# A first row map for the first two expert slots, ahead of the whole map of the routing

## The chip, the cores and the metric

The kernel runs on one core of a Trainium2 chip. The metric is the device time of one execution in microseconds (us). A core has a matrix engine (PE, with its weight loads shown apart as PEld), a vector engine (DVE), an activation engine (ACT), a general engine (POOL) and a queue engine (SP); each runs its own instructions in order and waits for the others on semaphores. Data comes from memory by 16 DMA engines.

## The reference

What matters here is the first stage, a mixture of experts (two of eight for each of 2048 tokens); a linear attention, an attention with a field and two local attention layers with feed-forward parts follow.

```python
x = x + attn(moe(x, cond_256))
x = x + ffn(cond2(x, cond_256))

def moe(x, genre_embed, rms_w, wg_W, wg_b, gg_W, gg_b, W1, b1, W2, b2, W3, b3):
    var = jnp.mean(x * x, axis=-1, keepdims=True)
    xn = rms_w * (x * jax.lax.rsqrt(var + EPS))
    gate = xn @ wg_W + wg_b + (genre_embed @ gg_W + gg_b)
    gate_w = jax.nn.softmax(gate, axis=-1)
    topk_w, topk_i = jax.lax.top_k(gate_w, TOP_K)
    cw = jnp.sum(jax.nn.one_hot(topk_i, E) * topk_w[..., None], axis=-2)
    h1 = jax.nn.relu(jnp.einsum('bsh,ehm->bsem', x, W1) + b1)
    h2 = jax.nn.relu(jnp.einsum('bsem,emn->bsen', h1, W2) + b2)
    out_e = jnp.einsum('bsen,enh->bseh', h2, W3) + b3
    return jnp.einsum('bseh,bse->bsh', out_e, cw)
```

x is 4 x 512 x 256, all in 32-bit floats; the experts are 256 to 512 to 512 to 256.

## The kernel before

The kernel doesn't compute every expert for every token. It sorts the 4096 choices (2048 tokens, two choices k each) into slots, each of one or two rows of 128 tokens of one expert, and runs the slots one after another (18 that always run, `often`, and 6 under a condition).

*Routing.* After the gate's products (PE, to 16.9 us) DVE finds the two choices of each token, counts them by expert, and works out for every choice its place: `slots`, split into `hl`, the place's upper part (`hl[:, 0]`, which 64 rows) and lower part (`hl[:, 1]`, which of the 64). `eid` holds the expert of each slot. The *row map* turns this around: for each place, the token that sits there. It is made by PE as a product of one-hots, in four groups of four tiles of 128 tokens (lines 1412 to 1432): on DVE `ol` (L1417, comparing the lower part with 0 to 63) and `oh` (L1422, comparing the upper part with 0 to 79), then `ol` is multiplied by the token's number, for k = 0 on ACT (L1426), for k = 1 on DVE (L1427). PE multiplies `ol` (its 64 columns are the weights) with `oh` (80 columns moving) and sums over the tiles into `pmap`; k = 0 goes to the rows 0 to 63 of the result and k = 1 to 64 to 127. Then the sum is copied (L1434), folded over k by PE (`mfold`, L1437), and turned into `rowtok`, token numbers (L1439, L1440), and `goal`, where results are to be written (L1442, L1445). `busy(n)` issues n products that nobody reads (n x 2 MATMULs of 512 columns).

*Slots.* `loads(j)` reads the expert number from `eid` on SP and starts the slot's weights: w1 (516 KB), w2 (1024 KB), w3 (640 KB); there are two buffers of each, so the first two slots' loads start at once, and slot j + 2's when slot j is done with its weights. `fetch(j)` gathers the slot's rows of x by `rowtok` with an indirect DMA on POOL, one for each 128 tokens. `turn_tokens` transposes them on PE and copies them on ACT into `xbT`. `layer` is one expert layer: products on PE into `ph`, then bias and relu, in turn on ACT (L1459) and DVE (L1461). Slot 0 has one row of 128 tokens, slot 1 two. A slot of one row makes its four quarters m = 0 to 3 of a layer in one bank and only then runs the four relus.

*The order of the work.* A framework orders the instructions and sets the semaphores. Instructions given to `pinned` (`keep_in_program_order`), and PE's inside `PE.in_order()`, keep the order of the program on their engine. In the loop over the slots, iteration j does: layer one of slot j, loads of slot j + 1, gathers of slot j + 2 (for j = 0 `xtail` too), layer three of slot j - 1, the scatters of results, the transposes of slot j + 1, layer two of slot j. Before the loop stand slot 0's loads, the gathers of slots 0 and 1, and slot 0's transposes.

Of the kernel before, what the change touches and what calls it, by code (L numbers as in the profile page):

```python
# [67 lines left out]
def adaln_attn_ffn_kernel(ctx: ExitStack, tc: tile.TileContext, a: dict, out: bass.AP):  # L68
# [1105 lines left out]
    with ExitStack() as abc:  # L1174
# [7 lines left out]
        with ExitStack() as moe:  # L1182
# [140 lines left out]
            PE.matmul(ppos[:, :128], tot, mtiles[:, :128], start=False, stop=True)  # L1323
            E2 = [128, NE, 3 * NE]
# [74 lines left out]
            nc.vector.tensor_copy(hl, hli)  # L1399
            past = per_expert("past")  # L1400
# [10 lines left out]
            nc.vector.tensor_copy(nhalf, halfs[0:1, NE - 1 : NE])  # L1411
            pmap = acct("pmap")
            for i0 in range(0, B * NT, 4):
                i1 = i0 + 4
                O4 = [128, 2, 4, 64]
                ol = hp.tile(O4, F32, tag="ob", name="ol", bufs=3)
                nc.vector.tensor_tensor(  # L1417
                    ol, hl[:, 1, :, i0:i1].unsqueeze(3).to_broadcast(O4),
                    miota[:, :64].unsqueeze(1).unsqueeze(1).to_broadcast(O4), ALU.is_equal)
                H4 = [128, 2, 4, NHI]  # L1420
                oh = hp.tile(H4, F32, tag="h1", name="oh")
                nc.vector.tensor_tensor(  # L1422
                    oh, hl[:, 0, :, i0:i1].unsqueeze(3).to_broadcast(H4),
                    miota.unsqueeze(1).unsqueeze(1).to_broadcast(H4), ALU.is_equal)
                for i in range(i0, i1):
                    nc.scalar.mul(ol[:, 0, i - i0, :], ol[:, 0, i - i0, :], mtok[:, i : i + 1])  # L1426
                nc.vector.tensor_tensor(  # L1427
                    ol[:, 1], ol[:, 1], mtok[:, B * NT + i0 : B * NT + i1].unsqueeze(2).to_broadcast([128, 4, 64]), ALU.mult)
                for i in range(i0, i1):
                    for k in range(2):  # L1430
                        PE.matmul(pmap[64 * k : 64 * k + 64, :NHI], ol[:, k, i - i0, :], oh[:, k, i - i0, :],
                                  start=(i == 0), stop=(i == B * NT - 1))
            half_map = xp.tile([128, NROWT, 2], F32, tag="hmap", name="hmap")
            nc.vector.tensor_copy(half_map, pmap[:, :NHI].rearrange("p (r q) -> p r q", q=2))  # L1434
            pmap2 = acct("pmap2")
            for q in range(2):
                PE.matmul(pmap2[64 * q : 64 * q + 64, :NROWT], mfold, half_map[:, :, q], start=True, stop=True)  # L1437
            rowtok = xp.tile([128, NROWT], I32, tag="rowtok", name="rowtok")
            nc.vector.tensor_scalar(rowtok, pmap2[:, :NROWT], -1.0, 0.0, ALU.add, ALU.max)  # L1439
            nc.vector.tensor_single_scalar(rowtok, rowtok, B * S - 1, op=ALU.bitwise_and)  # L1440
            goalf = xp.tile([128, NROWT], F32, tag="goalf", name="goalf")
            nc.vector.scalar_tensor_tensor(goalf, pmap2[:, :NROWT], 0.0, maside.to_broadcast([128, NROWT]),  # L1442
                                           ALU.is_equal, ALU.mult)
            goal = xp.tile([128, NROWT], I32, tag="goal", name="goal")
            nc.vector.tensor_tensor(goal, pmap2[:, :NROWT], goalf, ALU.add)  # L1445


            def busy(n):
                with PE.in_order():
                    ps = mmt("pbusy")  # L1450
                    for _ in range(n):
                        PE.matmul(ps, ident, xres[0].rearrange("p t h -> p (t h)")[:, :512], start=True, stop=True)


            busy(4)
# [12 lines left out]
            def loads(j, d):  # L1468
                e = nc.sync.value_load(eid[j : j + 1, 0:1], min_val=0, max_val=NE - 1)
# [16 lines left out]
            def fetch(j, d):  # L1486
                d.xb = hp.tile([128, 2, H], F32, tag="xb", name="xb", bufs=3)
                for i in range(d.n):
                    r = place(d.n, SLOTS[j][0]) + i
                    pinned(nc.gpsimd.indirect_dma_start(  # L1490
                        out=d.xb[:, i, :], out_offset=None, in_=xall,
                        in_offset=bass.IndirectOffsetOnAxis(ap=rowtok[:, r : r + 1], axis=0)))
# [30 lines left out]
            def layer(d, src, tag, w, bias):  # L1523
# [4 lines left out]
                for m2 in range(d.n):  # L1528
                    ps = mmt("ph")
                    k = 4 // d.n  # L1530
                    for i in range(k):
                        m = m2 * k + i
                        mm(ps[:, i * n : (i + 1) * n],
                           [(w[:, c, m * 128 : (m + 1) * 128], src[:, c, 0:n]) for c in range(w.shape[1])])
                    if d.n == 2:
# [135 lines left out]
            fetch(0, ds[0])  # L1671
            fetch(1, ds[1])
            with PE.in_order():
                turn_tokens(ds[0])
            last_wide = max(j for j, d in enumerate(ds) if d.wide)
            often, rare = ds[:-NRARE], range(len(ds) - NRARE, len(ds))
            for j, d in enumerate(often):
# [9 lines left out]
                with PE.in_order():  # L1687
                    if d.few:
                        h1 = layer_few(d, d.xbT, d.t1, "h1", w1, d.s1, 0)
                    else:  # L1690
                        h1 = layer(d, d.xbT, "h1", w1, 0)
                    if j + 1 < len(often):
# [11 lines left out]
                    if j == 0:  # L1704
                        pinned(nc.gpsimd.indirect_dma_start(
# [370 lines left out]
```

## Time and profile before

| | us |
|---|---|
| time, median of 3 runs (1340.82 to 1342.1) | 1341.5 |
| the profiled execution | 1343.32 |
| its span, first to last instruction | 1341.6 |
| PE busy in the span | 1271.8 |
| hl made (DVE) | 30.5 |
| slot 0's w1, w2, w3 started | 29.98, 30.55, 31.08 |
| slot 1's w1, w2, w3 started | 32.20, 32.79, 33.32 |
| map's products (PE) | 32.15 to 38.2 |
| filler on PE, busy(4) | 38.76 to 42.46 |
| gathers issued on POOL: slot 0, slot 1 (two), slot 2 (two), xtail | 39.58, 40.92, 42.20, 43.45, 44.70, 45.95 |
| slot 0's transposes, first layer, second layer | 45.21, 46.11, 49.42 |
| slot 1's first layer | 53.65 |

The profile is of one execution. Times in it count from the span's start. In the chain of waits each line is a start, a length, and the engine and line whose work the end hung on; a transfer's length there runs from its issue to its landing. An engine's idle time costs only where it is in this chain. PEclk is the clock granted to PE, 1.00 or 0.50 in this profile. A product of 32-bit floats shows as two MATMULs.

### The profile page before, as it was taken

What the parts mean: (1) busy time and instruction counts of PE and PEld (TensorE: products, weight loads), DVE (VectorE), ACT (ScalarE), POOL (GpSimd) and SP (SyncE); (2) the same over time, 40 slices, a digit from 0 to 9 for tenths busy, and PEclk for the clock granted to TensorE, in tenths of its full rate; (3) what the DMA queues carried; (4) which work ended last, traced back from release to release, by engine and by line L of the source; (5) the groups of instructions that cost most, each with busy time, mean ns of one, the idle gap of its engine ahead of it and who ended that gap; (6) DMA issues with size and microseconds to landing.
All of it is one profiled execution on the core that took longest, in us unless ns stands there. A gap on an engine that the chain in (4) does not pass through costs nothing.

```text
span 1341.6 us, 23073 instructions
## 1 busy us (share of the span) xinstructions
PE 1271.8 (95%) x9214; PEld 812.2 (61%) x9214; DVE 683.4 (51%) x1464; ACT 581.4 (43%) x1157; POOL 292.9 (22%) x321
## 2 busy tenths in 40 slices
PE   4899999998999999999999999999999998999998
PEld 3788899964566634344344655766555556667654
DVE  6221243425777733242237788654372877864421
ACT  3221233326655365646644646561222655463111
POOL 1322356420000101010103334210030333422010
PEclk7899999998999999999999999999999999999999
DMA  3565666523000000000210001311001011012000
GB/s 96 213 236 192 236 239 221 189 76 116 1 1 1 1 1 1 0 1 1 91 57 14 18 18 27 104 34 25 24 0 43 25 30 30 18 43 56 18 21 22
DMA packets 41856, 85.29 MB, mean 64 GB/s; under 512 B 9409, under 2 KB 25673, under 8 KB 39433
## 3 DMA queue, kind: packets, MB, share of 16 engines
q1 hardware_dynamic: 36600, 73.02, 16.9%
q0 software_dynamic: 3504, 9.46, 2.1%
q8 instruction: 77, 1.26, 0.4%
q10 hardware_dynamic: 1632, 1.21, 0.3%
q14 instruction: 43, 0.34, 0.1%
HBM read 74.76 MB, written 6.82 MB: 61 GB/s over the span
## 4 chain that ended last, share of the span: by engine, by line
PE 75%; DVE 9%; DMA 6%; ACT 5%; issue 3%; POOL 1%; SPq 0%; DVEq 0%; POOLq 0%
PE ph L82 11%; PE pdq L82 7%; PE pfy L82 6%; PE sc L82 6%; PE pua L82 5%; PE pug L82 5%; PE pv L82 5%; PE pdy L82 4%; PE po L82 3%; PE pn L82 3%; DMA ys<-ob,goal 2%; PE pds L82 2%; PE pqk L82 1%; PE pz L82 1%; PE pqt L86 1%
## 5 line engine op out<-in xcount | busy, mean ns | idle before, releaser
L82 PE MATMUL pdq<-wqkv,yT 128*128 128x512 f32 x384 | 171.7, 597 | 2.4 <-DVE t L626 2.2
L424 ACT ACTIVATE cex<-sc 128x512 f32<-128x512 f32 x256 | 132.2, 604 | 85.6 <-PE sc L82 84.6
L82 PEld LDWEIGHTS pdq<-wqkv,yT 128*128 128x128 f32 x384 | 71.1, 190 | 84.6 <-issue 76.1
L82 PE MATMUL ph<-h,w 128*128 128x256 f32 (+2 forms) x576 | 121.5, 370 | 0.3 <-ACT h L1596 0.3
L629 POOL TENSOR_TENSOR qr<-t,t 128x512 f32<-128x512 f32 x64 | 81.3, 1271 | 140.5 <-DVE t L626 140.5
L82 PEld LDWEIGHTS ph<-h,w 128*128 128x128 f32 x576 | 102.0, 192 | 15.2 <-ACT h L1596 0.5
L1461 DVE TENSOR_SCALAR h<-ph,w 128x256 f32<-128x256 f32 (+2 forms) x52 | 23.0, 461 | 121.8 <-PE ph L82 101.7
L394 POOL TENSOR_SCALAR fterm<-vw,faT 128x256 f32<-128x256 f32 x16 | 14.6, 920 | 317.6 <-DVE cr L384 317.6
L82 PE MATMUL sc<-qm,kT 32*128 32x512 f32 x512 | 82.6, 639 | 0.0
L681 ACT ACTIVATE p<-pds,ss 128x192 f32<-128x192 f32 (+1 forms) x256 | 79.8, 425 | 2.1 <-PE pds L82 0.8
L82 PE MATMUL pua<-hT,w 128*128 128x512 f32 x160 | 75.3, 593 | 0.9 <-DVE z L706 0.9
L82 PE MATMUL pug<-hT,w 128*128 128x512 f32 x160 | 76.2, 598 | 0.0
L619 ACT ACTIVATE sq<-pdq 128x512 f32<-128x512 f32 x64 | 38.5, 601 | 83.7 <-POOL qr L629 42.2
L714 POOL TENSOR_TENSOR p<-p 128x192 f32<-128x192 f32 x64 | 42.4, 682 | 138.1 <-PE pn L82 135.3
L796 ACT ACTIVATE gl<-pug,cols 128x512 f32<-128x512 f32 x40 | 27.3, 687 | 93.6 <-PE pug L82 90.8
L82 PE MATMUL pv<-cex,v 128*32 128x512 f32 x512 | 61.9, 598 | 2.7 <-DVE vw L391 2.7
L82 PE MATMUL pfy<-w,uA 128*128 128x256 f32 x256 | 61.4, 383 | 0.0
L82 PE MATMUL po<-w,h 128*128 128x256 f32 x264 | 60.1, 380 | 0.0
L82 PE MATMUL pdy<-wo,oT 128*128 128x256 f32 x256 | 58.9, 383 | 0.0
L684 DVE TENSOR_TENSOR p<-p,lmask 128x384 f32<-128x384 f32 x64 | 47.0, 735 | 23.0 <-ACT p L681 21.6
L82 PE MATMUL pn<-p,v 64*64 64x128 f32 (+1 forms) x1792 | 50.3, 254 | 8.2 <-DVE p L687 4.2
L1459 ACT ACTIVATE h<-ph,w 128x256 f32<-128x256 f32 (+2 forms) x52 | 22.4, 455 | 81.9 <-PE ph L82 78.0
(352 smaller groups left out, 2329.8 us busy)
## 6 DMA issues: line engine op xcount, KB each, us to landing
w<-in_moe_w_dram SPq DMA_DIRECT2D x18, 1024.0 KB, 7.9
w<-in_moe_w_dram SPq DMA_DIRECT2D x18, 516.0 KB, 4.0
w<-in_moe_w_dram SPq DMA_DIRECT2D x14, 640.0 KB, 4.5
zb<-rows SPq DMA_DIRECT2D x32, 256.0 KB, 4.1
g<-ys SPq DMA_DIRECT2D x6, 512.0 KB, 6.9
wqkv<-in_f_wqkv_dram SPq DMA_DIRECT2D x2, 1536.0 KB
w<-in_f_w_dram SPq DMA_DIRECT2D x2, 1408.0 KB
w<-in_moe_w_dram SPq DMA_DIRECT2D x4, 512.0 KB
```

Source lines behind the costliest of these rows:

```text
L82: cls._queue(nc.tensor.matmul(*args, **kw))
L86: cls._queue(nc.tensor.transpose(*args, **kw))
L394: nc.gpsimd.tensor_scalar_mul(fterm[:, t, :], vw, W["faT"][:, t, b : b + 1])
L424: nc.scalar.activation(ex[:, i, :], pss[2 * j + i], AF.Exp, scale=CHD**-0.5)
L619: nc.scalar.activation(sq, p3, AF.Square)
L629: nc.gpsimd.tensor_tensor(qr_t[:, s], t1, t2, ALU.add)
L681: nc.scalar.activation(p[:, j * 192 : j * 192 + n], pss[j // 2][r][:, j % 2 * 192 : j % 2 * 192 + n], AF.Exp, scale=d.ss[:, j, 1, 2 * c + ...
L684: nc.vector.tensor_tensor(edges, edges, lmask[:, :128].rearrange("p (s q) -> p s q", q=64).unsqueeze(1).to_broadcast([128, 3, 2, 64]), ALU ...
L714: nc.gpsimd.tensor_tensor(p[:, 1:, 0:64], p[:, 1:, 0:64], p[:, : NT - 1, 128:], ALU.add)
L796: nc.scalar.activation(gl, pg, AF.Gelu, bias=col("bg", l * (NU + 1) + i))
L1459: pinned(nc.scalar.activation(dst, src, AF.Relu, bias=bias))
L1461: pinned(nc.vector.tensor_scalar(dst, src, bias, 0.0, ALU.add, ALU.max))
```

## The change

- A *small map* is made first, for the three rows of slots 0 and 1 alone. `oh0` compares the upper part with the six values of these rows (two comparisons) and is itself multiplied by the token numbers, so that the lower one-hots `ols` can be used unscaled. `ols` is now made whole (four comparisons of 512 elements), in y[1] and y[3]. 32 products of six columns, k alternating, then copy, fold, `early_rows`, and the three gathers of slots 0 and 1.
- The *whole map* follows: `full_onehots` for the four groups (upper one-hots, scaling of `ols` in place on ACT and DVE), then the products of three groups, then slot 0's transposes, then those of the fourth group. Its copy stands before the loop, and the fold, `rowtok` and `goal` behind slot 0's first layer (`full_rows`), so the gathers of slot 2 and of `xtail` come after that.
- Almost all instructions of both maps are pinned to the program's order.
- `eids` is a copy of `eid` that depends on `early_rows` and stands behind the last whole-map one-hot on DVE; all slots but slot 0 read their expert from it, so their loads start behind it.
- Filler: `busy(7)` behind the counting products, `busy(2)` and `busy(1)` among the whole map's products; `busy(4)` goes.
- Slot 1's transposes move into slot 0's second layer, behind its third quarter.

```diff
@@ -1321,6 +1321,14 @@
 pcnt = mmt("pcnt")
 PE.matmul(pcnt[:, :NE], tot, mtiles[:, 128:], start=True, stop=True)
 PE.matmul(ppos[:, :128], tot, mtiles[:, :128], start=False, stop=True)
+def busy(n):
+    with PE.in_order():
+        ps = mmt("pbusy")
+        for _ in range(n):
+            PE.matmul(ps, ident, xres[0].rearrange("p t h -> p (t h)")[:, :512], start=True, stop=True)
+busy(7)
 E2 = [128, NE, 3 * NE]
 over = xp.tile(E2, F32, tag="over", name="over")
 nc.vector.tensor_tensor(over, pcnt[:, :NE].unsqueeze(2).to_broadcast(E2),
@@ -1397,6 +1405,7 @@
 nc.vector.tensor_single_scalar(hli[:, 1], slots, 63, op=ALU.bitwise_and)
 hl = xp.tile([128, 2, 2, B * NT], F32, tag="hl", name="hl")
 nc.vector.tensor_copy(hl, hli)
 past = per_expert("past")
 nc.vector.scalar_tensor_tensor(past, pairs, mslot[:, 0:1], mwt, ALU.is_le, ALU.mult)
 nc.vector.scalar_tensor_tensor(past, halfs, mslot[:, 1:2], past, ALU.is_le, ALU.add)
@@ -1409,50 +1418,98 @@
 nc.vector.tensor_scalar_min(eid, eidf, float(NE - 1))
 nhalf = xp.tile([1, 1], I32, tag="nhalf", name="nhalf")
 nc.vector.tensor_copy(nhalf, halfs[0:1, NE - 1 : NE])
+def one_hot(out, of, iota):
+    shape = list(of.shape) + [iota.shape[1]]
+    for _ in of.shape[1:]:
+        iota = iota.unsqueeze(1)
+    tc.keep_in_program_order(nc.vector.tensor_tensor(
+        out, of.unsqueeze(len(of.shape)).to_broadcast(shape), iota.to_broadcast(shape), ALU.is_equal))
+first = [2 * NPAIR + SLOTS[0][0], 2 * SLOTS[1][0], 2 * SLOTS[1][0] + 1]
+oh0 = y[2].rearrange("p t h -> p (t h)")[:, : 12 * B * NT].rearrange("p (k i n) -> p k i n", k=2, n=6)
+for at, r, n in ((0, first[0], 2), (2, first[1], 4)):
+    one_hot(oh0[:, :, :, at : at + n], hl[:, 0], miota[:, 2 * r : 2 * r + n])
+tokens = mtok.rearrange("p (k i) -> p k i", k=2)
+pinned(nc.vector.tensor_tensor(
+    oh0, oh0, tokens.unsqueeze(3).to_broadcast([128, 2, B * NT, 6]), ALU.mult))
+ols = [y[k].rearrange("p t h -> p (t h)").rearrange("p (i n) -> p i n", n=64) for k in (1, 3)]
+for i0 in (0, B * NT // 2):
+    for k in range(2):
+        one_hot(ols[k][:, i0 : i0 + B * NT // 2], hl[:, 1, k, i0 : i0 + B * NT // 2], miota[:, :64])
+def map_products(pmap, n, onehot, k, tiles):
+    for i in tiles:
+        PE.matmul(pmap[64 * k : 64 * k + 64, : 2 * n], ols[k][:, i, :], onehot(k, i),
+                  start=(i == 0), stop=(i == B * NT - 1))
+def map_copied(pmap, n):
+    half_map = xp.tile([128, n, 2], F32, tag=f"hmap{n}", name="hmap")
+    pinned(nc.vector.tensor_copy(half_map, pmap[:, : 2 * n].rearrange("p (r q) -> p r q", q=2)))
+    return half_map
+def map_rows(half_map, n):
+    pmap2 = acct("pmap2")
+    for q in range(2):
+        PE.matmul(pmap2[64 * q : 64 * q + 64, :n], mfold, half_map[:, :, q], start=True, stop=True)
+    rowtok = xp.tile([128, n], I32, tag=f"rowtok{n}", name="rowtok")
+    pinned(nc.vector.tensor_scalar(rowtok, pmap2[:, :n], -1.0, 0.0, ALU.add, ALU.max))
+    pinned(nc.vector.tensor_single_scalar(rowtok, rowtok, B * S - 1, op=ALU.bitwise_and))
+    return pmap2, rowtok
+def gather(dst, table, r):
+    pinned(nc.gpsimd.indirect_dma_start(
+        out=dst, out_offset=None, in_=xall,
+        in_offset=bass.IndirectOffsetOnAxis(ap=table[:, r : r + 1], axis=0)))
+with PE.in_order():
+    pmap = acct("pmap")
+    for i in range(B * NT):
+        for k in range(2):
+            map_products(pmap, 3, lambda k, i: oh0[:, k, i, :], k, [i])
+    early_rows = map_rows(map_copied(pmap, 3), 3)[1]
+xbs = [hp.tile([128, 2, H], F32, tag="xb", name="xb", bufs=3) for j in range(2)]
+gather(xbs[0][:, 0, :], early_rows, 0)
+for i in range(2):
+    gather(xbs[1][:, i, :], early_rows, 1 + i)
+eids = xp.tile([128, 1], I32, tag="eids", name="eids")
 pmap = acct("pmap")
-for i0 in range(0, B * NT, 4):
-    i1 = i0 + 4
...
-goal = xp.tile([128, NROWT], I32, tag="goal", name="goal")
-nc.vector.tensor_tensor(goal, pmap2[:, :NROWT], goalf, ALU.add)
+ohs = []
+def full_onehots(g):
+    tiles = slice(4 * g, 4 * g + 4)
+    oh = hp.tile([128, 2, 4, NHI], F32, tag=f"h{1 + g // 2}", name="oh")
+    one_hot(oh, hl[:, 0, :, tiles], miota)
+    for i in range(4 * g, 4 * g + 4):
+        pinned(nc.scalar.mul(ols[0][:, i, :], ols[0][:, i, :], mtok[:, i : i + 1]))
+    pinned(nc.vector.tensor_tensor(
+        ols[1][:, tiles], ols[1][:, tiles], tokens[:, 1, tiles].unsqueeze(2).to_broadcast([128, 4, 64]),
+        ALU.mult))
+    ohs.append(oh)
+def full_products(g):
     with PE.in_order():
-        ps = mmt("pbusy")
-        for _ in range(n):
-            PE.matmul(ps, ident, xres[0].rearrange("p t h -> p (t h)")[:, :512], start=True, stop=True)
-busy(4)
+        for i in range(4 * g, 4 * g + 4):
+            for k in range(2):
+                map_products(pmap, NROWT, lambda k, i: ohs[i // 4][:, k, i % 4, :], k, [i])
+for g in range(4):
+    full_onehots(g)
+pinned(nc.vector.scalar_tensor_tensor(eids, early_rows[:, 0:1], 0.0, eid, ALU.min, ALU.max))
+busy(2)
+for g in range(3):
+    full_products(g)
+    if g == 0:
+        busy(1)
+def full_rows():
+    pmap2, rowtok = map_rows(full_map, NROWT)
+    goalf = xp.tile([128, NROWT], F32, tag="goalf", name="goalf")
+    pinned(nc.vector.scalar_tensor_tensor(
+        goalf, pmap2[:, :NROWT], 0.0, maside.to_broadcast([128, NROWT]), ALU.is_equal, ALU.mult))
+    goal = xp.tile([128, NROWT], I32, tag="goal", name="goal")
+    pinned(nc.vector.tensor_tensor(goal, pmap2[:, :NROWT], goalf, ALU.add))
+    return rowtok, goal
 def relu(dst, src, bias):
     if turn[0]:
@@ -1466,7 +1523,7 @@
     return 2 * i if kind == 2 else 2 * NPAIR + i
 def loads(j, d):
-    e = nc.sync.value_load(eid[j : j + 1, 0:1], min_val=0, max_val=NE - 1)
+    e = nc.sync.value_load((eids if j else eid)[j : j + 1, 0:1], min_val=0, max_val=NE - 1)
     we = a["moe_w"][bass.DynSlice(e, 1)].rearrange("o p f -> (o p) f")
     d.w1 = ew.tile([128, 8 + 2 * ME], F32, tag="w1", name="w1")
     nc.sync.dma_start(d.w1, we[:, 0 : 8 + 2 * ME])
@@ -1487,9 +1544,7 @@
     d.xb = hp.tile([128, 2, H], F32, tag="xb", name="xb", bufs=3)
     for i in range(d.n):
         r = place(d.n, SLOTS[j][0]) + i
-        pinned(nc.gpsimd.indirect_dma_start(
-            out=d.xb[:, i, :], out_offset=None, in_=xall,
-            in_offset=bass.IndirectOffsetOnAxis(ap=rowtok[:, r : r + 1], axis=0)))
+        gather(d.xb[:, i, :], rowtok, r)
 def turn_tokens(d):
     n = d.n * 128
@@ -1520,7 +1575,7 @@
         relu(dst[:, m, :], ps, d.w1[:, bias + m : bias + m + 1])
     return dst
-def layer(d, src, tag, w, bias):
+def layer(d, src, tag, w, bias, between=None):
     if d.wide:
         return wide_layer(d, src, tag, w, bias)
     n = d.n * 128
@@ -1532,6 +1587,8 @@
             m = m2 * k + i
             mm(ps[:, i * n : (i + 1) * n],
                [(w[:, c, m * 128 : (m + 1) * 128], src[:, c, 0:n]) for c in range(w.shape[1])])
+            if between is not None and m == 2:
+                between()
         if d.n == 2:
             turn[0] ^= 1
         for i in range(k):
@@ -1668,10 +1725,12 @@
 btail = y[3][:, 0]
 htail = y[2].rearrange("p t h -> p (t h)")[:, 512:].rearrange("p (w c n) -> p w c n", w=NWIDE, c=4)
 loads(0, ds[0])
-fetch(0, ds[0])
-fetch(1, ds[1])
+ds[0].xb, ds[1].xb = xbs
 with PE.in_order():
     turn_tokens(ds[0])
+    full_products(3)
+with PE.in_order():
+    full_map = map_copied(pmap, NROWT)
 last_wide = max(j for j, d in enumerate(ds) if d.wide)
 often, rare = ds[:-NRARE], range(len(ds) - NRARE, len(ds))
 for j, d in enumerate(often):
@@ -1689,6 +1748,8 @@
             h1 = layer_few(d, d.xbT, d.t1, "h1", w1, d.s1, 0)
         else:
             h1 = layer(d, d.xbT, "h1", w1, 0)
+        if j == 0:
+            rowtok, goal = full_rows()
         if j + 1 < len(often):
             loads(j + 1, after)
             for name in list(later)[: (j > 1) + (j > 8)]:
@@ -1702,9 +1763,7 @@
         if j + 2 < len(often):
             fetch(j + 2, ds[j + 2])
         if j == 0:
-            pinned(nc.gpsimd.indirect_dma_start(
-                out=xtail, out_offset=None, in_=xall,
-                in_offset=bass.IndirectOffsetOnAxis(ap=rowtok[:, TAILS : TAILS + 1], axis=0)))
+            gather(xtail, rowtok, TAILS)
         if j == last_wide + 3:
             scatter_tails()
         if j:
@@ -1717,9 +1776,9 @@
         if 9 < j < 10 + B:
             pinned(nc.gpsimd.tensor_tensor(
                 xres[j - 10], xres[j - 10], row("bo").unsqueeze(1).to_broadcast([128, NT, H]), ALU.add))
-        if j + 1 < len(often):
+        if 0 < j < len(often) - 1:
             turn_tokens(after)
-        d.h2 = layer(d, h1, "h2", d.w2, 4)
+        d.h2 = layer(d, h1, "h2", d.w2, 4, None if j else lambda: turn_tokens(after))
         if d.wide:
             pinned(nc.scalar.copy(htail[:, d.at], d.h2[:, :, 256:]))
 last(len(often) - 1, often[-1])
```

## The prediction

> **What bounds the kernel now.** I read the page's engine table first: PE is busy 95% of the span, so time can only be had where PE waits or runs at a low clock. The slices' clock row shows one such place, slices 1 and 2.
>
> ```profile
> PE 1271.8 (95%) x9214; PEld 812.2 (61%) x9214; DVE 683.4 (51%) x1464; ACT 581.4 (43%) x1157; POOL 292.9 (22%) x321
> PEclk7899999998999999999999999999999999999999
> ```
>
> The chain that ended last, in order of time, tells what sets the end there.
>
> ```profile
> 30.57 0.69 DVE ol L1417
> 31.26 0.74 DVE oh L1422
> 32.00 0.33 DVE ol L1427
> ...
> 37.16 1.03 PE pmap L82 x16
> 38.19 0.02 issue
> 38.21 0.25 DVE hmap L1434
> ...
> 39.58 5.59 DMA xb<-in_x_dram,rowtok
> ...
> 46.11 2.66 PE ph L82 x16
> 48.77 0.85 PE pxb L86 x4
> 49.63 7.64 PE ph L82 x48
> ```
>
> The reader sees one line of dependence: one-hots on DVE, map products on PE, the gather of slot 0's tokens (5.59 us), and only then slot 0's first layer at 46.11. After that the chain is PE alone until 170 us, so what is won at 46.11 is kept. Third, busy time and granted clock by stretch (columns: stretch, its length, then PE, PEld, DVE, ACT, POOL busy, clock, DMA share, GB/s).
>
> ```profile
> 20.10:23.80 3.70, 2.17 (x8) 1.86 (x8) 2.61 (x12) 0.42 (x2) 0.00 (x0) 0.50 0.00 0
> 23.80:32.10 8.30, 0.00 (x0) 0.00 (x0) 8.06 (x51) 0.80 (x4) 0.00 (x0) 0.50 0.13 25
> 33.80:37.20 3.40, 3.18 (x33) 2.77 (x34) 3.40 (x7) 2.12 (x9) 0.00 (x0) 0.51 1.00 411
> 37.20:42.50 5.30, 4.92 (x28) 2.37 (x28) 0.93 (x6) 0.24 (x2) 2.31 (x3) 1.00 1.01 418
> 42.50:45.20 2.70, 0.00 (x0) 0.00 (x0) 0.00 (x0) 0.00 (x0) 2.09 (x3) 1.00 0.53 165
> 47.30:50.70 3.40, 3.40 (x19) 3.40 (x18) 0.70 (x2) 1.21 (x3) 0.00 (x0) 0.51 0.14 39
> ```
>
> PE is idle from 23.8 to 32.1, works the map at half clock, and after the idle 2.7 us before the gather lands it runs at half clock again from 47.3 to 50.7. The gather travels while the DMA engines are full (share 1.01) with two slots' weights.
>
> **The change part by part**, as times on this trace.
>
> *Small map.* After hl (ends 30.5): a 64-element and a 128-element comparison and a 192-element product. Rows: 0.29 (128 elements), 0.36 (192), the first between 0.17 (16 elements) and 0.29, so 0.23; the first two overlap by 0.08: 0.8, to 31.4. Then four 512-element one-hots at the pitch 0.61 that L1417 shows, the last taking 0.69: the first pair is ready at 32.7, the last at 33.9. 64 MATMULs of six columns follow, 32 for each half. The trace has no such shape. Nearest is pmap<-oh,ol with the same 64-column weights, also alternating: 14 MATMULs in 37.5 to 38.0 at clock 1.00, 0.036 each; the upper bound is 16 in 1.57 at clock 0.50, 0.098 (that time holds waits). I take 0.036: first half done at 33.85, second 33.9 to 35.05, plus 0.23 of the last one's own length: 35.3. Copy, fold, rowtok and its AND took 38.21 to 39.29, 1.08, to 36.4; the gather begins 0.17 after its last operand: 36.5, 3.1 earlier than 39.58.
>
> [...]
>
> *Filler.* busy(7) is 14 MATMULs from 23.8 on. At clock 1.00 the present filler has a pitch of 0.43; at 0.50 I take 0.86, twice, because ph shows 12 MATMULs in 2.35 us at 0.50 and 25 in 2.50 at 1.00. The clock rose after 3.4 us of work (33.8 to 37.2) or, counting the sparser start, 5.1 (32.1 to 37.2). So 4 to 6 of the 14 run slowly and the filler ends at 31.5 to 32.3, before the products at 32.7: no cost, and full clock for them. Without a rise it ends at 35.8 and costs its overhang.
>
> *Gather's flight.* The 33 gathers land after 2.7 / 3.3 / 6.1 us (least, median, most); this one took 5.59 among weights. Now only slot 0's weights are under way, 2.18 MB at about 410 GB/s from 31.3 on, 5.3 us, over at about 37. I take the median: landed at 39.8; bounds 39.2 and 42.6.
>
> *The whole map moves behind.* DVE stands still from 33.9 to 35.3, since the map's copy is pinned and waits for PE; everything pinned after it waits too. From 36.4 come four times 0.74 + 0.34 (L1422 and L1427 at their pitch), 4.3, to 40.7, then eids, 0.15. ACT's 16 scalings (1.06 for four, 4.2 in all) follow the small products, 35.3 to 39.5, ahead of slot 0's token copy; that isn't late. PE after the fold (35.9): busy(2) 1.7, to 37.6; first quarter of the products 16 x 0.036 = 0.6, to 38.2; busy(1) 0.86, to 39.0; second to 39.6; third, ready at 39.6, to 40.2; transposes 0.45 to 40.65, with the gather already there; the last quarter waits for DVE until 40.7 and ends at 41.4. The token copy ends at 41.1 (0.02 + 0.38 + 0.04 after the transposes). First layer: 41.4 instead of 46.11, **4.7 earlier**. DVE's 4.3 us set this, not the gather, which has about 0.4 us in hand.
>
> *Slot 0's two layers* took 46.11 to 53.65, 7.54, of which 3.4 at half clock. At full clock: 16 MATMULs x 0.11 = 1.8; then the four relus one after another (48.81 to 50.35, 1.54, 0.2 after PE) with only the fold between, because slot 1's transposes, which filled this place, move behind the third quarter of layer two. Its first quarter so ends at 3.8, then 24 x 0.11 + 4 x 0.11 = 3.1: 6.9, **0.6 less**. Without the clock's drop before, the moved transposes would be a loss of about 0.4.
>
> *Slot 1's and 2's data.* SP took 1.03 from eid to the first transfer: 41.9. w1 lands 4.0 later, 45.9, needed at 41.4 + 6.9 = 48.3. w2 (42.5) lands after 7.9, at most 10.2: 50.4 to 52.7, needed 5.6 later than slot 1's start, 53.9. POOL issues slot 2's gathers when the whole rowtok is made, behind the first layer's relus, at about 45.3 and 46.6 instead of 43.45 and 44.70, and xtail at 47.9; by the worst row the second lands at 52.7, needed at 53.5. Behind them POOL has slot 2's weight sums, due at about 54; SP has nothing until slot 2's weights. So these moves cost nothing, with margins of 2.4, 1.2 and 0.8.
>
> **Sum.** 4.7 + 0.6 = 5.3. The profiled execution took 1343.3 (span 1341.6 and 1.7 around it), so 1338.0 for it; it stands 1.8 above the median 1341.5, from which the forecast is **1336.2**.
>
> **The rivals.**
>
> *The clock drops between filler and whole map.* For: the drop at 20.1 came after 3.2 idle us, the one at 47.3 after a gap of 2.7 and sparse work; nothing here shows whether six-column products hold the clock. Against: the pause after the filler is 1.2 at most. If it halves from 34 to 41: second half 3.1 instead of 1.15, gather at 38.5, DVE done at 42.7, first layer at 43.5; 2.6 + 0.6 = 3.2 gained: 1338.3.
>
> *POOL can't issue the gathers beside DVE's one-hots.* In this trace every DVE operation that overlaps a gather's issue reads PSUM, so it is bounded: nothing, or until DVE is done at 40.7, landing 3.3 later at 44.0, first layer 44.9: 1.2 + 0.6, 1339.7. I take nothing, as the issues beside PSUM readers last 0.94 to 1.03 with and without them.
>
> [...]
>
> *Slot 1's or 2's data come late.* Each margin above spent, every further microsecond costs one: with 5 us of lateness nothing is left, 1341. Against it: all three worst rows were seen with two slots' weights under way, and now one is.
>
> *The filler gets in the way (the slower side).* It is in PE's queue ahead of the products. If the clock doesn't rise during it, it holds PE to 35.8, the products take 64 x 0.098 = 6.3, to 42.1, the gather starts at 43.5, the second filler and the quarters run at half clock and the first layer starts at about 55, 9 later, its layers 3.5 longer: 1354. The break-even is a rise at about 39: then the products end at 40.1, DVE at 45.7, the first layer starts at 46.4. Against: 14 dense MATMULs, and both rises in the trace came within 3.4 to 5.1 us of work.
>
> **How the numbers follow.** Forecast (own range 1334 to 1338) 0.60; clock drop 0.12; POOL held 0.10; late data 0.06; slower 0.12. Range 1332.8 to 1342.0: below, a clock that never drops again later; above, it takes in the gaining rivals and no loss, and leaves out the slower case with a little at either end. 0.2% is 2.7 us, what the measurement can tell from no change: faster means under 1338.8. Forecast, most of the clock drop and a third of POOL's case: 0.73. The rest of these and late data: 0.14. Slower, with a little for a queue order unlike the one read from the code: 0.13.
>
> **What would show it.** First gather issued near 36.5 and landed near 40; clock 1.00 without a break from 27 to 31 on; PE's first layer at 41 to 42; slot 1's at 48 to 49. Wrong if the gather's issue outlasts 1.1 us or flies over 5 beside the one-hots, if the granted clock shows 0.50 after 33, if PE waits for w1 or xb of slots 1 and 2, or if DVE's whole-map stretch exceeds 4.3 us.

## The result, and the profile after

The changed kernel takes **1344.86 us** (median of 21 runs, 1339.94 to 1348.62) against 1341.19 for the kernel before beside it (21 runs, 1335.94 to 1342.16): 1.0031 times as long, 95% interval 1.0022 to 1.0040. The forecast was 1336.2, faster. The profiled execution took 1347.1, its span is 1345.4.

From the page of the changed kernel, the engine table, the slices' clock row and the chain's shares by engine:

```profile
PE 1283.2 (95%) x9294; PEld 816.6 (61%) x9294; DVE 685.2 (51%) x1471; ACT 581.8 (43%) x1157; POOL 292.0 (22%) x321
PEclk8999999999999999999999999999999999989999
PE 72%; DVE 10%; DMA 9%; ACT 4%; issue 3%; POOL 1%; SPq 0%; DVEq 0%; POOLq 0%
```

PE has 80 MATMULs and 80 weight loads more. DMA holds 9% of the chain; before it was 6%: more of the end is set by transfers, though a gather was taken off it.

The chain around the change, in order of time (start, length, what):

```profile
31.34 2.42 DVE ymoe L1426 x4
33.76 0.04 issue
33.80 1.11 PE pmap L82 x30
...
35.44 3.18 PE pbusy L82 x4
38.62 1.07 PE pmap L82 x16
39.70 1.06 PE pbusy L82 x2
...
42.38 0.70 PE pmap L82 x16
43.08 2.00 PE ph L82 x16
```

The gather's wait is gone from the chain and slot 0's first layer starts at 43.08 instead of 46.11; slot 1's starts at 50.1 instead of 53.65. So the change does what it is for: 3.5 us are gained. They are still there 600 us later, and then they are lost in a part of the kernel that the change does not touch, the two local attention layers. There SP issues transfers that are waited for: `sums`, `rden`, `rows` and `zb` take the attention's sums through memory and back (8 KB each, `zb` 256 KB), `hn` brings rows of the tokens for the normalization (the one in the chain is 30 KB), and `pua` is a product that follows. The same chain there, first of the kernel before, then of the changed one:

```profile
805.89 2.36 DMA hn<-yc
...
862.99 7.96 DMA zb<-rows
...
872.93 1.99 PE pua L82 x4
```

```profile
802.05 4.13 DMA hn<-yc
...
861.02 9.29 DMA zb<-rows
...
872.28 3.63 PE pua L82 x4
...
915.49 2.87 DMA rows<-rden
```

The same transfers, issued in the same order, take longer to land (hn by 1.8 us, zb by 1.3), the rows transfer at 915 is new on the chain, and the products behind zb run at half clock. The busy table of 780 to 930 us (columns as before the change: length, PE, PEld, DVE, ACT, POOL, clock, DMA share, GB/s), first before, then after:

```profile
780.00:930.00 150.00, 144.17 (x1585) 95.97 (x1570) 108.81 (x257) 78.78 (x164) 42.34 (x45) 1.00 0.18 47
```

```profile
780.00:930.00 150.00, 142.23 (x1484) 93.97 (x1481) 104.54 (x247) 76.84 (x161) 39.23 (x43) 0.98 0.18 46
```

The mean clock is 0.98 instead of 1.00 (two falls to 0.50 of 3.4 us each, at 810.8 and 872.2), and in the same 150 us PE does 1484 MATMULs instead of 1585.

### The profile page after: what moved, and what is told of

Read it like the earlier page. It is cut to its first block, busy times and chain, and to the rows that moved or that the text cites. A ratio compares the mean times of both kernels' runs of the same rounds, so it can differ in the third digit from the quotient of the medians.

```text
span 1345.4 us, 23252 instructions
## 1 busy us (share of the span) xinstructions
PE 1283.2 (95%) x9294; PEld 816.6 (61%) x9294; DVE 685.2 (51%) x1471; ACT 581.8 (43%) x1157; POOL 292.0 (22%) x321
## 4 chain that ended last, share of the span: by engine, by line
PE 72%; DVE 10%; DMA 9%; ACT 4%; issue 3%; POOL 1%; SPq 0%; DVEq 0%; POOLq 0%
PE ph L82 11%; PE pdq L82 6%; PE sc L82 6%; PE pfy L82 5%; PE pua L82 5%; PE pv L82 5%; PE pug L82 5%; PE pdy L82 4%; PE po L82 3%; PE pn L82 2%; DMA zb<-rows 2%; DMA ys<-ob,goal 2%; PE pqt L86 2%; PE pqk L82 1%; DVE t L626 1%
## 5 line engine op out<-in xcount | busy, mean ns | idle before, releaser
L82 PEld LDWEIGHTS pn<-p,v 64*64 64x64 f32 x1792 | 45.4, 138 | 20.5 <-issue 11.5
```

Source lines behind the costliest of these rows:

```text
L82: cls._queue(nc.tensor.matmul(*args, **kw))
```

## The experiments

**What could do this.** The order of instructions of every engine is the same from slot 2 on. Three theories: *B*, the code's place: the change adds 161 instructions to PE's stream (80 + 80 and a wait), and what follows lies elsewhere against the packets of the instruction queue q8 (below). *K*, the clock: its falls last 3.4 us or a multiple of it (3.4, 6.8, 10.2 and 17.1 us in these profiles, but for the one at the end of each), and a stage that begins 4 us earlier may meet them differently. *A*, the tiles' addresses.

For B the trace has a row that the prediction did not use. Queue q8, which the page calls `instruction`, carries 77 packets of 16 KB, one for some 250 TensorE rows (MATMULs, weight loads and waits; medians of 255 and 252.5 rows from packet to packet in the two profiles, with some records missing). From that name and this count I take a packet for the fetch of a block of TensorE's code, and the expectations put a block at 256 rows; no run shows what a packet holds, and whether it costs anything is what is on trial. The DMA queues (packets, MB, share of the 16 engines) while hn is under way, in the changed kernel from 801.9 to 806.3 us, and in the first experiment from 802.3 to 804.9:

```profile
q1 hardware_dynamic: 547, 0.27, 25.4%
q8 instruction: 1, 0.02, 2.3%
q14 instruction: 1, 0.01, 0.6%
```

```profile
q1 hardware_dynamic: 539, 0.26, 41.3%
q14 instruction: 1, 0.01, 0.8%
```

One q8 packet more: it starts 0.7 us after hn's issue and takes 1.64 us.

### Moving the code, and nothing else (e1 to e4)

Products of one column, whose result nobody reads, in PE's wait of 16.8 to 21.5 us: 24 times in e1, 40 in e2 and e4, 64 in e3, four rows each. So e1 has 257 rows more than before, about one block, and e2 has 160 more, where the changed kernel has 161.

```diff
             ptot = mmt("ptot")
-            PE.matmul(ptot[:, 0:1], flat, ones, start=True, stop=True)
+            with PE.in_order():
+                for _ in range(24):
+                    PE.matmul(ptot[0:1, 64:65], ident[:, 0:1], ident[:, 0:1], start=True, stop=True)
+                PE.matmul(ptot[:, 0:1], flat, ones, start=True, stop=True)
```

> The changed kernel with 24 one-column products put into a PSUM column that nobody reads, at 16.6 us, where TensorE waits for the top-2 choice until 21.5 us: 96 rows more on TensorE (a product is two weight loads and two matmuls), so 161 + 96 = 257 rows more than before. Theory B (blocks of code): queue q8 fetches one block of 16 KB for each 256 TensorE rows in both traces; the change moves the places of these fetches by 161 of 256 rows, and they fall on the short DMAs that the local attention layers wait for (a fetch of 1.64 us at 802.8 us beside the hn load that took 4.13 instead of 2.36 us, one of 1.74 us at 860.5 beside the zb loads of 9.29 instead of 7.96 us). With 257 rows the fetches stand where they stood before, so the 4.2 us that the change is ahead at 690 us stay: 1337 us, 0.996 to 0.998 of before. Theory K (clock windows alone: a stage that starts 4 us earlier meets other windows, whatever the code): no difference from the changed kernel, 1345 us, 1.003. Theory A (addresses of the tiles): the same as K, 1345 us.

> The kernel before with 40 such products at the same place, 160 rows more on TensorE, hidden in its wait for the top-2 choice. Theory B: its code blocks end where those of the changed kernel do (161 rows more), the short DMAs of the local layers become late and the clock drops follow: 1341.2 + 6 to 8 = 1347 to 1349 us, 1.0045 to 1.006. Theory K: the local stage begins at the same time as before, so 1341 us, 1.000. Theory A: 1341 us too.

> The changed kernel with 64 such products, 256 rows: one whole block more. Control for the filling itself (its activity, its time). Theory B: the blocks end where those of the changed kernel end, 1345 us, 1.003. If the padding as such took away the loss (say by keeping the clock up at 18 us), this one would be as quick as the one with 24: 1337 us. Theories K and A: 1345 us. Should the 64 products last beyond 21.5 us, up to 1 us more in all three.

> The changed kernel with 40 such products, 161 + 160 = 321 rows, that is 65 beyond the place of before: a phase of the blocks that no kernel had yet. Theory B: some time of its own between the two, 1335 to 1348 us, with its hn, zb and rows loads late where a q8 fetch stands beside them, and not elsewhere. Theories K and A: 1345 us, as the changed kernel.

Measured beside one another (before 1338.9): the changed kernel with its code where before's lies (e1) 1336.4, ratio 0.9987, interval 0.9973 to 1.0000. The kernel *before* with its code where the changed one's lies (e2) 1346.4, 1.0057 (1.0034 to 1.0079). One whole block more (e3) 1341.0, 1.0025 (1.0009 to 1.0041), as the changed kernel. A fourth place (e4) 1338.9, 1.0007 (0.9993 to 1.0022); in its profile another hn load, at 864.6, is on the chain with 5.45 us, and a q8 packet starts 0.1 us before it.

K and A expected no difference from moving the code, and fall: e2 has the routing and tiles of before, and within 1.0 us the start of its local stage, and loses 7.5 us. Filling as such is no cure either, as e3 shows. The chain of e2 at the places shown above:

```profile
863.68 9.59 DMA zb<-rows
...
875.25 2.95 PE pua L82 x4
...
918.31 3.16 DMA rows<-rden
```

And e1's, again in the same places:

```profile
802.41 2.37 DMA hn<-yc
...
859.42 7.96 DMA zb<-rows
...
869.35 1.98 PE pua L82 x4
```

In e2 the transfers of the changed kernel have come back with the clock's fall behind them; in e1 all is as before, and the rows transfer at 915 is off the chain. In seven of the profiles, the time of the transfer on the chain and the starts of q8's packets after its issue (from the packet records; "-": not on the chain):

```
code lies as       kernel   hn             zb                    rows at 915
before's           before   2.36 none      7.96 (+5.3)           -
                   e1       2.37 none      7.96 (+6.6)           -
                   e12      2.34 none      8.61 (+5.0)           -
the changed one's  changed  4.13 (+0.7)    9.29 (-0.5, +7.6)     2.87 (+0.9)
                   e2       4.25 (+0.7)    9.59 (+1.2, +7.6)     3.16 (+0.8)
                   e3       3.96 (+0.7)    9.08 (+2.0, +7.6)     2.65 (+0.4)
                   e14      -              10.29 (+2.6, +7.8)    -
```

Rows without a fetch takes 1.40. zb is the weakest witness: it travels beside a 1536 KB weight load, and with one late fetch and no early one e7's took 9.13 and e9's 9.21. Over the chains of all 16 profiles after 690 us, hn took 2.33 to 2.42 us in the 27 cases with no q8 packet under way, and 2.84 to 5.77 in the nine with one; the two longest are e4's and e8's, issued 5.4 us after that weight load. Rows took 1.39 to 1.41 in 51 cases without and 2.65 to 3.16 in three with. But not every transfer suffers: sums took 1.69 to 1.76 in all 61 cases, 45 of them with a packet under way, and rden was longer only in the two of 25 whose packet started after its issue (2.66 and 3.03, the others 1.51 to 1.81). A late transfer is also likelier to be on the chain: off it, with its packet 2.0 us after the issue, one of the changed kernel's hn took 2.31.

Where the time goes, as the start of the same matmul less its start in the profile of before (us; columns e9, e12 and e14 are told of below):

```
start before   changed   e2      e3      e14     e1      e9      e12
  63.0          -3.47   +0.62   -1.46   -4.87   -1.63   -3.13   -4.60
 664.8          -4.21   -0.69   -1.11   -6.07   -3.15   -6.76   -9.19
 784.9          -3.85   -1.02   -2.53   -7.63   -3.48   -8.04  -10.84
 965.4          +2.36   +5.15   +0.84   -2.71   -3.57   -6.90  -10.36
1266.2          +4.22   +5.16   +0.37   -3.57   -6.30   -8.14  -13.50
```

Between 784.9 and 965.4 the four whose code lies as the changed kernel's lose 6.2, 6.2, 3.4 and 4.9 us; the others -0.1, 1.1 and 0.5, and the eight profiles that are not in the table 0.1 to 1.5. e3's clock does not fall in this stretch, so its 3.4 us are lost without the clock. The changed kernel has two falls besides (shown here), e2 and e14 one each:

```profile
872.20:875.60 3.40, 3.32 (x4) 1.51 (x5) 3.00 (x16) 1.67 (x3) 0.00 (x0) 0.50 0.03 5
810.80:814.20 3.40, 3.40 (x20) 2.85 (x19) 2.94 (x6) 3.40 (x10) 2.92 (x2) 0.50 0.32 94
```

What it loses after 965 goes with a fall of 6.8 us at 1189.6, where before has 3.4. The rows at 63 and 665 also hold each execution's own falls of the clock (near 303, for one, 10.2 us in before and 3.4 to 6.8 in the others).

### What the early gain lost (e5 to e8)

All with the code where before's lies, but for e6, whose blocks end 32 rows sooner (14 one-column products at 16.8 us; e5 has 22). e5 and e6: busy(8) for busy(7), and one more product between the halves of the small map's loop

```diff
+                return ps
...
-            busy(7)
+            filler = busy(8)
...
                 for i in range(B * NT):
+                    if i == B * NT // 2:
+                        for _ in range(1):
+                            PE.matmul(filler, ident, xres[0].rearrange("p t h -> p (t h)")[:, :512], start=True, stop=True)
                     for k in range(2):
```

> The changed kernel with its code blocks where those of before are (22 one-column products, and 8 rows more from filling: 257 rows as with 24), and with more filling around the small map: 8 filler products in place of 7 ahead of it, and one between its two halves, so that TensorE works from 31 to 34 us, where it waited for the one-hots. Step on trial: my forecast lost 1.6 us of its early gain because the clock fell to 0.50 at 35 us (first layer at 43.0 us, forecast 41.4), and with the padding, whose windows lie 1 to 2 us earlier, 6.8 us long (first layer at 44.9). If the thin stretch of the small map is what lets it fall, there is no 0.50 between 33 and 42 us now, the first layer starts at 41.5 to 42 us, and the total is 2 to 3 us under that of the kernel with 24 products alone: 0.996 to 0.997 of before. If the one-hots of the whole map on VectorE or something else make it fall, or the filling counts for nothing: a drop at 34 to 36 us as there, first layer at 43 to 45 us, 0.9987. If the filler is itself in the way (one product is 0.85 us at full clock), the small map ends later than 35.5 us and 0.5 us are lost.

> The same with 14 one-column products: 225 rows, blocks that end 32 rows sooner than before's. Theory B: the fetches move by some 32 rows, one to two us, against the short DMAs of the local layers; in the trace of the kernel with 24 this takes the fetch counted at the critical DMAs from 8 to 6, so the same or up to 2 us quicker than the one with 22, 0.994 to 0.997 of before; any late hn, zb or rows load has a q8 fetch beside its issue. Theory K: the same as with 22.

e5 1338.1, 0.9990 (0.9978 to 1.0003); e6 1338.35, 0.9989 (0.9976 to 1.0003). In e6's profile the clock stays at 1.00 from 27.2 to 300 us and the first layer starts at 42.7; in e5's it falls at 36.8 for 3.4 us, and the layer starts at 44.4. The third outcome came true as well: the product sits in the way, and the small map's last product ends at 36.2 in both, against 34.9 in the changed kernel, whose one-hots begin 0.4 us sooner. No gain in time, and what brings the clock down stays open.

e7 takes the small map's products of the first choice first, then the second's:

```diff
-                for i in range(B * NT):
-                    for k in range(2):
-                        map_products(pmap, 3, lambda k, i: oh0[:, k, i, :], k, [i])
+                for i0 in (0, B * NT // 2):
+                    for k in range(2):
+                        map_products(pmap, 3, lambda k, i: oh0[:, k, i, :], k, range(i0, i0 + B * NT // 2))
```

> The kernel with 24 products, and of the small map in each half first the eight products of the first choice, then the eight of the second, not in turn. If taking turns is what makes a product short (0.036 us a MATMUL in the changed kernel, the weights of one loading while the other runs in the other half of the array), a MATMUL and its load now take more, 0.05 us or above at full clock: 1.5 us and more in place of 1.1 for 30 of them, the small map 0.4 us or more later. If not: 0.036 us each at full clock, twice that at 0.50, and no difference in time from the kernel with 24, 0.9987.

Timelines, e7's weight loads and then the changed kernel's second half:

```profile
32.00 3.74 PEld L82 LDWEIGHTS pmap<-ymoe,ymoe 128*64 128x64 f32 x64 [1.11 <-PE pbusy L82]
```

```profile
33.80 1.01 PEld L82 LDWEIGHTS pmap<-ymoe,ymoe 128*64 128x64 f32 x30 [0.19 <-DVE ymoe L1426]
```

64 loads take 3.74 us here, 30 take 1.01 there, with the same clock until 34.5. By the starts of the single MATMULs, those of one half follow at 0.058 us (0.107 at half clock), and in the changed kernel a pair follows a pair at 0.058, 0.029 each. So taking turns halves a MATMUL's time. The map's end moves by less: eight products of one choice run while the other's one-hots are made, and counted from the first of these one-hots the map ends 0.2 us later than e1's (4.56 against 4.34 us; the clock falls in both before the end). 1340.15, 1.0001 (0.9985 to 1.0017), unclear against e1.

e8 reads all expert numbers from the first table:

```diff
-                e = nc.sync.value_load((eids if j else eid)[j : j + 1, 0:1], min_val=0, max_val=NE - 1)
+                e = nc.sync.value_load(eid[j : j + 1, 0:1], min_val=0, max_val=NE - 1)
```

> The kernel with 24 products, and all slots' weights loaded by the first table of expert numbers (eid), not by the copy that waits for the whole map's one-hots: slot 1's three loads are issued 4 to 5 us sooner. My forecast gave nothing for that wait. If it was right: slot 1's first layer and the rest at the same time, 0.9987. If the loads sooner are in the way of the small map's gathers: these land 0.5 us or more later, and slot 0's first layer with them; total up to 0.5 us more. If slot 1 waited for its weights: its first layer comes sooner, up to 0.5 us less.

1337.8, 0.9985 (0.9971 to 1.0000), as e1. But slot 1's loads go out at 32.66 instead of 42.33, and the gather is on e8's chain again:

```profile
36.66 7.48 DMA xb<-in_x_dram,rowtok
```

That is slot 0's. Of the third gather the trace tells the landing in both: 6.6 us here, 3.3 in e1, so the wait behind the one-hots is what keeps the gathers short. It shows in no total; a likely reason is that in e1 PE, with its filler at half clock, begins the first layer hardly sooner: 44.9 against e8's 45.3.

### The gain kept (e9 to e12), and two controls (e13, e14)

e9 leaves the changed kernel alone until 711 us and moves the code only there, where PE waits for the first scaled queries (in e9 `tiny` is 22 and `big` 2):

```diff
                     pt = mmt("pqt")
+                    if t == s == 0 and tiny + big:
+                        PE.pinned = True
+                        for _ in range(big):
+                            PE.matmul(pt, ident, xres[0].rearrange("p t h -> p (t h)")[:, :512], start=True, stop=True)
+                        for _ in range(tiny):
+                            PE.matmul(pt[0:1, 0:1], ident[:, 0:1], ident[:, 0:1], start=True, stop=True)
...
+                    if t == s == 0 and tiny + big:
+                        PE.pinned = False
```

> The changed kernel, whose code is its own until 711 us, and then 24 products that nobody reads (22 of one column, 2 of 512) in the place of the first local layer where TensorE waits from 711 to 715.3 us for the scaled queries: 96 rows more from there on. Theory B (the fetches of TensorE's code): the loss comes from the place of the fetches in the local layers alone, so all that the change gains until 690 us is kept (2 to 4 us, by how long the clock falls at 35 us) and 1 to 2 us come to it: 1335 to 1338 us, 0.996 to 0.9985 of before; hn at 802 us lands in 2.4 us, not 4.1, and no q8 fetch stands beside the zb loads at 860 us. If it was not the fetches in the local layers but something that the early padding changed (the clock at 18 us, the code of the routing), the loss stays: 1345 us, 1.003.

> The one before with 9 filler products ahead of the small map in place of 7 (and 22 late products in place of 24), so that TensorE works until 32.5 us, when the first half's one-hots are ready. If the pause from 30.8 to 32.1 us is what brings the clock down at 35 us, the first layer comes at 41.5 to 42 us instead of 43 to 45 us and the total is 1 to 2 us under the one with 7: 0.995 to 0.9975. If the short six-column products after it are enough to bring it down, no difference: the drop at 34 to 36 us stays, 0.996 to 0.9985. If the ninth product is in the way: the first half 0.3 us later, no gain.

> The same change with the two fillers behind the small map left out, busy(2) and busy(1) (and 27 late products): the whole map's products start when their one-hots and scalings are there, 37 to 38 us, instead of behind the filler at 38.6 to 40.5. If the filler, which takes 3.2 to 3.7 us when the clock is down, is what the path waits for: first layer at 41.5 to 42.5 us although the clock falls, total 0.5 to 2 us under the one with filler. If without it the clock falls for longer, and into slot 0's first layer: that layer, 2.0 us at full clock, takes 3 to 4 and the total is 1 to 3 us above.

> Both at once: 9 filler products ahead of the small map, none behind it, and 25 late products (23 of one column, 2 of 512), 257 rows more than before from 711 us on. If the two add up: the first layer at 41.5 to 42 us as without the filler, the code of the local layers where it does no harm, 0.995 to 0.9965 of before, the quickest so far. If the nine are of no use once the filler behind is gone: as the one without, 0.9974. If TensorE, with no filler behind the small map, keeps 0.50 into slot 0's layers (2.0 us at full clock, 4.0 at half): 0.998 to 1.000.

Against before: e9 0.9983 (0.9970 to 0.9997), e10 0.9962 (0.9948 to 0.9976), e11 0.9974 (0.9963 to 0.9985), e12 0.9964 (0.9949 to 0.9978; 1334.3 us, its profile's span 1327.7). All four are faster than before, and after 711 us none differs from the changed kernel but by the place of its code and that filling. Without the filler behind the small map (e11) the chain reads:

```profile
33.41 3.70 ACT ymoe L1492 x15
...
37.20 3.58 PE pmap L82 x48
...
41.16 0.70 PE pmap L82 x16
41.86 2.00 PE ph L82 x16
```

First layer at 41.86, 1.55 sooner than in e9, though the clock falls at 37.1 all the same: ScalarE's scalings and the products themselves set it now, not the filler, and the clock is back before the layer. The nine filler products of e10 gain nothing in the routing (first layer 43.56, the fall at 36.8 stays), so that its total lies below e9's, with overlapping intervals, is no proof for them.

Two controls ask what the late filling does by itself. e13 gives its two long products to the kernel before; e14 is e12 without the late products.

> The kernel before with the two 512-column products alone in TensorE's wait of 711 to 715 us (8 rows, so its code blocks move by 8 of 256). If the late filling itself makes the quickest kernels quick (TensorE busy there, no fall of the clock at 715 us), it gives the kernel before the same: 1 to 2 us less, 0.9985 to 0.9993 or below. If their gain is the change's with the code blocks in a harmless place: 1.000, within 0.05%.

> The quickest kernel (9 filler products ahead of the small map, none behind it) without its 25 late products: 161 + 8 - 12 = 157 rows more than before, so its code blocks end where those of the changed kernel do, and the routing is the quickest one's to the instruction. Theory B: the loss of the local layers is back, 5 to 8 us more than the quickest: 1340 to 1343 us, 1.0005 to 1.003. If the better filling of the routing made it quick and not the place of the code: 1335 to 1337 us, 0.9965 to 0.998 (the late filling's own part lost, no more).

e13 0.9997 (0.9984 to 1.0010): no gain from the filling. e14 1341.0, 1.0015 (0.9999 to 1.0031): the loss is back, 0.5% between it and e12. Its chain, then e12's:

```profile
856.25 10.29 DMA zb<-rows
...
868.53 2.67 PE pua L82 x4
```

```profile
851.99 8.61 DMA zb<-rows
...
862.57 1.98 PE pua L82 x4
```

## Why the forecast was wrong

**The step that failed** is the sentence "After that the chain is PE alone until 170 us, so what is won at 46.11 is kept". It looked 120 us ahead in a program of 1340. Later the chain runs again through short transfers that SP issues (hn, sums, rden, rows, zb), in the profile of before as well, and some of these land later when TensorE's code lies elsewhere (hn after 4.13 us instead of 2.36 in the changed kernel, 4.25 in e2). No rival held this; all four looked at the routing. The added instructions had a cost outside their own stage: 6.2 us from 785 to 965 us, in a term that the sum did not have. Shown: moving the code alone makes the loss in the kernel before (e2, 1.0057) and takes it away in the changed one (e1, 0.9987). Seen with every late hn, rden and rows on the chain, but not shown by itself: that it is the q8 packet beside a transfer that delays it. No run leaves a packet out alone. How a late transfer is followed by a fall of the clock is not shown either; e3 lost 3.4 us with none. By what path one 16 KB packet would hold a transfer up for 1 to 2 us is open.

**The gain, point by point.**
- Filler ahead of the products: out of the way at 30.8 (forecast 31.5 to 32.3). The slower-side rival, a filler that holds PE to 35.8, did not occur.
- Small map: last one-hots at 33.76 (33.9), 30 MATMULs in 1.11 us, gather issued at 36.13 (36.5). Right, and the trace's 0.036 held; the products take turns there, and in e7, where they don't, one took 0.058.
- Gather: issued beside the one-hots in 1.35 us, later ones in 1.05 and 1.47; two of the three are over the 1.1 that I had named. It was no matter: the gathers of 30 to 60 us whose landing the trace tells took 2.7 to 3.6 us (slot 0's is not among them, but PE has no wait for it). The POOL rival had the direction (0.94 to 1.03 us in the kernel before) and not the size; that the one-hots lengthen the issue is not shown by itself.
- VectorE's whole map: 35.76 to 40.1 (36.4 to 40.7). Right. ScalarE's scalings ran from 32.4 to 36.6, beside the small products and not behind them (35.3 to 39.5).
- **First layer: 43.08, not 41.4.** Here the rival "the clock drops between filler and whole map" is what happened: 0.50 from 35.9 to 39.3, and busy(2) took 3.18 instead of 1.7. In e11 the layer starts at 41.86 with the fall, so the mis-sized term is the filler, which I had costed as cover and which is on the path when the clock falls: busy(2) and busy(1) took 4.24 us instead of 2.56, and that is the 1.7 us by which the layer is late. The clock by stretch in the changed kernel:

```profile
32.10:35.00 2.90, 2.44 (x64) 2.17 (x64) 1.71 (x4) 2.41 (x10) 0.00 (x0) 1.00 1.01 395
35.70:39.10 3.40, 3.40 (x12) 1.18 (x12) 3.40 (x8) 0.92 (x4) 2.40 (x2) 0.54 0.55 209
39.10:43.00 3.90, 3.90 (x64) 2.71 (x62) 1.09 (x3) 0.37 (x1) 1.47 (x1) 0.97 0.47 112
```

- Slot 0's two layers: 43.08 to 50.13, 7.05 (6.9). Slots 1 and 2 were not late. Right.

Together 3.5 us instead of 5.3 at slot 1; e12, without the filler behind the small map and with its code elsewhere, gains 0.36% of 1339.7, 4.8 us. So nearly the forecast gain was there to be had, by a different kernel. The range missed because its upper end was made of mishaps of the routing alone. One reading was short, too: the clock row of before shows a third low slice, the tenth, with a fall of 10.2 us at 303.4, and the prediction counted slices 1 and 2 alone.

## What to carry to other kernels

A change that adds instructions to an engine moves all code behind it, here by 161 rows of TensorE's. Where a later stage waits for short transfers, look at the instruction queue's packets beside them, before and after, and move the code by a few dozen products that nobody reads (both kernels, and one whole block as control) before judging a change of under 1% by its time: here the place of the code alone was worth 0.57% of the kernel before (e2). Follow the chain to the end of the program before calling a gain kept. A filler that is to keep the clock up is work in the queue like any other: ask what it costs if the clock falls in spite of it (here 4.24 us instead of 2.56).

## What the runs showed of the hardware

- SP's issue of a zb load takes 0.59 to 0.75 us in all 477 cases (16 profiles) in which no q8 packet is under way; of 35 in which one is, 18 take longer, up to 1.63 us. Beside the hn load at 802 to 805 us the packet itself takes 1.4 to 1.8 us, against medians of 1.0 to 1.1 over each profile.
- One kernel's runs spread in part with its mean clock: the changed kernel's 21 from a span of 1338.2 at 0.992 to 1346.8 at 0.987, the correlation of span and clock being -0.74.
- MATMULs with 64-column weights follow at 0.058 us within one half of the output rows and at 0.029 on average when the halves alternate, both at clock 1.00 (e7 and the changed kernel).
- The clock fell at 34 to 37 us in all profiles of the changed kernel and its variants but e6's, although in the changed kernel, where it fell at 35.9, PE was busy for 2.44 of the 2.9 us from 32.1 to 35.0, with six-column products. What brings the clock down there, and what would keep it up, is open.
